# One residual sum moved from VectorE to TensorE and ScalarE in the last rows, and one bank read moved behind weight sums at the start

## The chip, the cores and the metric

The kernel runs on one core of one Trainium2 chip. The metric is device time in microseconds (us) of one execution; each kernel was run several times, and the profiles are of single executions on the same kind of chip. A profile's span is about 1.8 us shorter than the time that the same execution is given (2750.9 against 2752.65), so spans are compared with spans and times with times.

## The reference

128 graphs of 64 nodes with 768 features go through a layer norm and a ReLU, then two layers of attention over the graph, and the input is added at the end. Cut to what matters:

```python
h = jnp.maximum(_layernorm(x, axis=-1), 0.0)
for l in range(2):
    m_left  = jnp.einsum('bsh,oh->bso', h, W_left[l])
    m_right = jnp.einsum('bsh,oh->bso', h, W_right[l])
    u_left  = jnp.einsum('bih,bjh->bij', h, m_left) / temper
    u_right = jnp.einsum('bih,bjh->bij', h, m_right) / temper
    # ... choose left or right by the triangle, exp, mask, divide by the row sum -> attention
    h_lin = jnp.einsum('bsh,oh->bso', h, W_lin[l]) + b_lin[l]
    ctx   = jnp.matmul(attention, h_lin)
    h     = jax.nn.relu(_layer_norm(ctx, ln_a[l], ln_b[l]))   # (z - mu) / (sigma + eps) * a + b
return x + h                                                   # all float32
```

## The kernel before

Every big projection (768 x 768 weights) is done by fifteen block products in place of eighteen (3 x 3 weight blocks times 2 token halves): sums of weight blocks are multiplied with sums of token blocks, and each product is added with a sign into several blocks of the result. A bank (X, Y, Z, V or aux here) is a piece of PSUM, the memory that the products are written to. The graphs go through in blocks. At the very start the weight sums aren't ready, so block 0 makes them just in time on VectorE; the dictionary `just` says which sums are made after which product.

```python
def read(p, to, i, seen, copied=nc.scalar):        # PSUM bank -> result blocks of product i
    what = ORDER[i][3]
    for n in range(0, len(what), 2):
        sign, o = what[n], int(what[n + 1])
        if o not in seen:                            # first contribution: ScalarE copies
            seen.add(o)
            nc.scalar.activation(to(o), p, AF.Copy, scale=1.0 if sign == "+" else -1.0)   # [cut]
        else:                                        # later ones: VectorE adds
            added(nc.vector, to(o), sign, to(o), p)

# start of the program: GpSimd makes the first two weight sums, VectorE the others
for f in ws[:2]:
    f()
t, w = deque(sums_t((1, 0, 0), nc.vector)), deque(vs[2:])
needs = ("twtwt", "ttwww", "wwww", "w", "tw", "t", "ww", "ww", "tt", "", "tt")   # t: token sum, w: weight sum

def project(u, k, just):
    # [cut]
    for i, (at, t, _) in ...:                        # fifteen products
        # [cut: four matmuls, eight records in a trace, into bank `at`]
        read(p, lambda o: M[u][...], i, seen)
        for f in just.get(i, ()):
            f()
        run(30 * k + 2 * i + 1)
```

The second product (`i == 1`) goes to bank Z, and four sums ("wwww") follow its read in VectorE's queue.

The other place is the end. The last 256 rows are two tiles, k=1 and k=0, of 128 rows by 768 columns. For each, the context is normalised and clipped into `zs[k]`, added to the residual `xs[k]` (with the bias `b` already in it), and stored in two halves of 64 rows on two DMA queues.

```python
def finish_last(u, r):
    cx = context(u, r)                               # last products of the program, into PSUM
    # [cut]
    for k in (1, 0):
        nc.scalar.activation(squares[:, k]..., cx[k], AF.Square, accum_out=ss[k])
        nc.vector.tensor_tensor(zs[1 - k]..., cx[1 - k], rows["a"]..., op=ALU.mult)
        nc.scalar.activation(rs[k], ss[k], AF.Sqrt, bias=floor, scale=1.0 / (H - 1.0))
    for k in (1, 0):
        nc.vector.tensor_scalar_add(rs[k], rs[k], EPS_LN)
        nc.vector.reciprocal(rs[k], rs[k])
        nc.vector.scalar_tensor_tensor(zs[k], zs[k], rs[k], rows["-b"], op0=ALU.mult, op1=ALU.max)
        nc.vector.tensor_add(xs[k], xs[k], zs[k])
        for h, queue in enumerate((nc.sync, nc.scalar)):
            queue.dma_start(out[u * NBB + batch(r, k, h)], xs[k][h * S:(h + 1) * S])
```

Of the kernel before, what the change touches and what calls it, by code (L numbers as in the profile page):

```python
# [10 lines left out]
F32 = mybir.dt.float32  # L11
# [6 lines left out]
def kernel(  # L18
# [24 lines left out]
    nc = tc.nc  # L43
    B, S, H = x.shape
    L = w_lin.shape[0]
    P = 128
    C = H // P
    HH = H // 2
# [5 lines left out]
    TH = T // 2  # L54
# [10 lines left out]
    ps_st = ctx.enter_context(tc.tile_pool(name="ps_st", bufs=1, space=bass.MemoryType.PSUM))  # L65
# [11 lines left out]
    def put(slot, *fs):  # L77
        plan.setdefault(slot, []).extend(fs)
# [8 lines left out]
    def run(slot):  # L87
        if slot in plan:
            for f in plan.pop(slot):
                f()  # L90
        elif idle:
            f = idle.popleft()
            if f is not None:
                f()
# [59 lines left out]
    def added(eng, o, sign, a, b):  # L154
        (eng.tensor_add if sign == "+" else eng.tensor_sub)(o, a, b)  # L155
# [13 lines left out]
    def tokens_of(key):  # L169
        ht = HT[key]  # L170
        r = {f"B{2 * j + t}": ht[:, j * K2:(j + 1) * K2, t * TH:(t + 1) * TH] for j in range(3) for t in range(2)}
        r.update(TS.get(key, {}))
        return r
# [19 lines left out]
    def read(p, to, i, seen, copied=nc.scalar):  # L193
# [4 lines that stand above are left out]
            if o not in seen:  # L198
                seen.add(o)
                if copied is nc.vector:  # L200
                    nc.vector.tensor_scalar_mul(to(o), p, 1.0 if sign == "+" else -1.0)
                    continue
                nc.scalar.activation(to(o), p, AF.Copy, scale=1.0 if sign == "+" else -1.0)  # L203
            else:
                added(nc.vector, to(o), sign, to(o), p)
# [17 lines left out]
    KEEP = {}  # L223
# [168 lines left out]
    def pass_one(l, aside):  # L392
        with tc.tile_pool(name=f"one{l}", bufs=2, reuse_waits="tile") as sp:
# [26 lines left out]
            def project(u, k, just):  # L420


                b, w = lambda: tokens_of((1, l, u)), W[l, "lr"[k]]
                bank, seen = {}, set()


                ns = S - 1 if k and u < NB - 1 else S
                bs = "p (b s) -> p b s"
                for i, (at, t, _) in ((i, (o[1], o[2], o[3])) for i, o in enumerate(ORDER)):
                    new = i in FIRST  # L430
                    if new:
                        bank[at] = ps_st.tile([P, 2 * TH], F32, name=at)
                    p = bank[at][:, :NBB * ns].rearrange("p (g b s) -> p g b s", g=2, s=ns)
                    for g in range(2):
                        for c in range(K2):
                            nc.tensor.matmul(p[:, g], w[ORDER[i][0]][:, c, g * P:(g + 1) * P],  # L436
                                             b()[t][:, c, :].rearrange(bs, s=S)[:, :, :ns],
                                             start=(new and g == c == 0), stop=(c == K2 - 1), skip_group_check=True)
                        if g == 0:
                            run(30 * k + 2 * i)  # L440
                    if i == 0 and k == 0:
                        if u:
                            scores(u - 1)
                        M[u] = sp.tile([P, C, NBB, 2, S], F32, name="m", bufs=1)
                    read(p, lambda o: M[u][:, o // 2 * K2:(o // 2 + 1) * K2, o % 2 * 4:o % 2 * 4 + 4, k, :ns],
                         i, seen)
                    for f in just.get(i, ()):
                        f()
                    run(30 * k + 2 * i + 1)

# [53 lines left out]
            just = {}  # L504
# [130 lines left out]
    def pass_two(l, aside):  # L635
        last = l == L - 1
        with tc.tile_pool(name=f"two{l}", bufs=2, reuse_waits="tile") as sp:
# [12 lines left out]
            def context(u, r):  # L650


                hl, at = HL[u], AT[u]
                lo, hi = slice(0, S), slice(S, P)
                cx = [ps_aux.tile([P, 2, T], F32, name="aux") for _ in range(2)]
                for n in range(2):
                    for (j, k, i) in ((lo, 0, lo), (hi, 0, hi), (lo, 1, hi), (hi, 1, lo)):
                        q = r + 2 * k
                        m = n if j == lo else 1 - n
                        nc.tensor.matmul(cx[k][i, m, :HH], at[j, q, :], hl[j, q, m * HH:(m + 1) * HH],  # L660
                                         start=True, stop=True)
                return [c[:, :, :HH] for c in cx]
# [23 lines left out]
            def batch(r, k, h):  # L686
                return 4 * (h if k == 0 else 1 - h) + r + 2 * k
# [3 lines left out]
            def last_block(u):  # L691


                rest = big.tile([P, C, T], F32, name="ht").rearrange("p c t -> p (c t)")
                rows["-b"] = sp.tile([P, H], F32, name="nb", bufs=1)
                for r in range(2):
                    XS[u, r] = [rest[:, n * H:(n + 1) * H] for n in (2 * r, 2 * r + 1)]

                def load(r):
                    for k in range(2):  # L700
                        for h in range(PAIR):
                            nc.sync.dma_start(XS[u, r][k][h * S:(h + 1) * S], x[u * NBB + batch(r, k, h)])

                put(1, lambda: load(1))
                put(6, lambda: nc.gpsimd.tensor_scalar_mul(rows["-b"], rows["b"], -1.0))
                put(20, lambda: load(0))

                def offset():

                    t = stat.tile([P, 1], F32, name="hold", bufs=1)  # L710
                    nc.gpsimd.tensor_copy(t, XS[u - 1, 1][1][:, :1])
                    for xs in XS[u, 1]:
                        nc.gpsimd.tensor_add(xs, xs, rows["b"])

                put(42, offset)

            def finish_last(u, r):


                cx = context(u, r)  # L720
                zs = [sp.tile([P, H], F32, name="z", bufs=4) for _ in range(2)]
                squares = sp.tile([P, Q, H], F32, name="hl", bufs=2)
                two = "p (n d) -> p n d"
                xs = XS[u, r]
                of = stat.tile([P, 2, 2], F32, name="of", bufs=1)
                ss, rs = ([of[:, n, k:k + 1] for k in range(2)] for n in range(2))
                for k in (1, 0):
                    nc.scalar.activation(squares[:, k].rearrange(two, n=2), cx[k], AF.Square, accum_out=ss[k])
                    nc.vector.tensor_tensor(zs[1 - k].rearrange(two, n=2), cx[1 - k],
                                            rows["a"].rearrange(two, n=2), op=ALU.mult)  # L730
                    nc.scalar.activation(rs[k], ss[k], AF.Sqrt, bias=floor, scale=1.0 / (H - 1.0))
                for k in (1, 0):
                    nc.vector.tensor_scalar_add(rs[k], rs[k], EPS_LN)
                    nc.vector.reciprocal(rs[k], rs[k])
                    nc.vector.scalar_tensor_tensor(zs[k], zs[k], rs[k], rows["-b"], op0=ALU.mult, op1=ALU.max)
                    nc.vector.tensor_add(xs[k], xs[k], zs[k])
                    for h, queue in enumerate((nc.sync, nc.scalar)):
                        queue.dma_start(out[u * NBB + batch(r, k, h)], xs[k][h * S:(h + 1) * S])
                return []
# [134 lines left out]
            for u in range(NB):  # L874
# [21 lines left out]
                else:  # L896
                    if turn:
                        load_h(1, 1, 0)
                        put_all(28, affine(1, 1, 0), 3)
                        put_sums_t((1, 1, 0), 38, 2, 30)  # L900
                        ends = ({1: ((u - 1, 0), (13, 14, 16)), 11: ((u - 1, 1), (34, 35, 36))},
                                {4: ((u, 0), (50, 51, 52))})
                    else:
                        last_block(u)
                        put(8, lambda: residual(u - 1, 1))
                        ends = ({0: ((u - 1, 0), (12, 13, 15, 19, 31)), 9: ((u - 1, 1), (28, 29, 30, 39, 41))},
                                {2: ((u, 0), (44, 48, 51, 61, 62))})
# [54 lines left out]
```

## Time and profile before

| | before |
|---|---|
| time, median of 4 runs | 2751.59 us (2750.17 to 2751.72) |
| profiled span | 2750.9 us |
| TensorE idle before the fifth product of block 0 | 1.48 us |
| first product of block 0 to its fifth | 9.44 us |
| end of the last context product to end of the span (the tail) | 10.57 us |
| in the tail: tile 1's stores issued, VectorE done, last byte | 4.26, 6.54, 9.38 us from its start |

The profile is read as places. TensorE is busy in 99% of the span, so a change that doesn't touch TensorE's work can only win where TensorE is not busy. The busy time by stretches of the kernel before shows the two places of this change. The columns are the stretch in us from the span's start, its length, then the busy time (and the instructions) of TensorE, weight loads, VectorE, ScalarE and GpSimd, then the granted clock, the DMA share and GB/s:

```profile
12.80:72.00 59.20, 56.86 (x385) 49.39 (x386) 40.22 (x63) 19.21 (x37) 26.81 (x22) 1.00 0.70 187
...
2740.30:2750.90 10.60, 0.00 (x0) 0.00 (x0) 6.32 (x11) 2.28 (x6) 0.00 (x0) 0.68 0.56 148
```

The first row is the first block's projection: TensorE is idle for 2.3 of its 59.2 us. The second is the tail: TensorE does nothing, VectorE works for 6.3 of 10.6 us, the rest is waiting and transfers.

In a timeline line, the first two numbers are when a group of instructions starts and how long it lasts. Then come the engine (PE is TensorE, PEld its weight loads, DVE VectorE, ACT ScalarE, POOL GpSimd; SPq and ACTq are the stores and loads issued by SyncE and ScalarE), the source line, the operation, output and inputs, shapes and count; the bracket gives the idle time of that engine just before and what ended it. A line number such as L155 can be that of a helper that all sums share.

### The profile page before, as it was taken

To read this page: it belongs to the slowest core of one execution; us is meant where nothing else is said; L and a number is where in the kernel's file an instruction comes from. 1 tells how busy PE (TensorE), PEld (TensorE's weight loads), DVE (VectorE), ACT (ScalarE), POOL (GpSimd) and SP (SyncE) were. 2 spreads that over 40 slices of the span, in tenths; PEclk is the share of its full clock that TensorE was granted. 3 is DMA by queue.
4 is the path that set the end of the run, shared out by engine and by line. 5 is a ranking of instruction groups with operands and counts; after the bars stand their busy time and mean duration, and the time that the engine had idled before them with its cause. 6 is when DMAs were issued, how large, how long until landed. Compare 5 with 4: busy or idle time off the path is not lost.

```text
span 2750.9 us, 46440 instructions
## 1 busy us (share of the span) xinstructions
PE 2730.4 (99%) x18746; PEld 2343.1 (85%) x18746; DVE 1345.6 (49%) x2266; ACT 849.9 (31%) x1612; POOL 1194.4 (43%) x937
## 2 busy tenths in 40 slices
PE   9999999999999999999999999999999999999998
PEld 8888888888888888888788888888888888888886
DVE  6555445545454333333435444444444335666667
ACT  3222223222221154444621211121122214544443
POOL 3332452223223555555522444223222325887886
PEclk9999999999999999999999999999999999999999
DMA  7434433343332333343555433443344205555555
GB/s 206 118 75 98 123 80 81 91 120 89 76 79 74 102 106 119 119 146 127 150 128 148 100 76 76 109 118 79 76 97 120 61 26 146 161 169 167 169 165 150
DMA packets 234072, 310.82 MB, mean 113 GB/s; under 512 B 54146, under 2 KB 184450, under 8 KB 225666
## 3 DMA queue, kind: packets, MB, share of 16 engines
q1 hardware_dynamic: 233698, 307.45, 41.8%
q8 instruction: 149, 2.44, 0.4%
q14 instruction: 65, 0.53, 0.1%
q10 hardware_dynamic: 160, 0.39, 0.0%
HBM read 202.91 MB, written 104.86 MB: 112 GB/s over the span
## 4 chain that ended last, share of the span: by engine, by line
PE 97%; DVE 1%; ACT 1%; DMA 0%; issue 0%; SPq 0%; DVEq 0%; ACTq 0%
PE X L436 24%; PE V L436 16%; PE X L852 12%; PE Y L436 12%; PE Z L436 8%; PE V L852 8%; PE Y L852 6%; PE aux L463 5%; PE Z L852 4%; PE aux L660 2%; PE aux L683 1%; PE Y L683 0%; ACT xb L316 0%; DVE wm L477 0%; DMA w_l<-in_w_left_dram 0%
## 5 line engine op out<-in xcount | busy, mean ns | idle before, releaser
L155 POOL TENSOR_TENSOR ts<-ht 128x512 f32<-128x512 f32 x441 | 587.0, 1341 | 1223.6 <-DMA ht<-h 565.1
L203 ACT ACTIVATE m<-X 128x512 f32<-128x512 f32 (+1 forms) x256 | 151.6, 592 | 1087.6 <-PE X L436 569.7
L155 POOL TENSOR_TENSOR ts<-ht,ts 128x512 f32<-128x512 f32 x189 | 248.7, 1323 | 135.6 <-PE X L852 60.5
L155 DVE TENSOR_TENSOR m<-m,V 128x512 f32<-128x512 f32 (+1 forms) x256 | 173.3, 677 | 269.1 <-PE V L436 269.0
L155 DVE TENSOR_TENSOR m<-m,X 128x512 f32<-128x512 f32 (+1 forms) x256 | 162.9, 677 | 248.0 <-PE X L436 247.4
L852 PE MATMUL X<-w_n,ts 128*128 128x256 f32 x1024 | 244.3, 380 | 0.8 <-ACT hl L203 0.6
L436 PE MATMUL X<-ts,w_l 128*128 128x256 f32 x1024 | 242.7, 380 | 0.1
L436 PE MATMUL X<-ts,w_r 128*128 128x252 f32 (+1 forms) x1024 | 238.8, 376 | 0.0
L155 DVE TENSOR_TENSOR m<-m,Z 128x512 f32<-128x512 f32 (+1 forms) x128 | 87.5, 683 | 307.7 <-ACT m L203 248.9
L852 PEld LDWEIGHTS X<-w_n,ts 128*128 128x128 f32 x1024 | 191.5, 190 | 33.3 <-issue 3.6
L436 PEld LDWEIGHTS X<-ts,w_l 128*128 128x128 f32 x1024 | 192.0, 190 | 30.1 <-DVE m L155 2.7
L436 PEld LDWEIGHTS X<-ts,w_r 128*128 128x128 f32 x1024 | 192.0, 190 | 26.0
L275 ACT ACTIVATE ht<-ht,b_col,a_col 128x512 f32<-128x512 f32 x192 | 143.5, 804 | 148.8 <-DMA ht<-h 148.8
L852 PE MATMUL Y<-w_n,ts 128*128 128x256 f32 x768 | 182.5, 379 | 0.0
L436 PE MATMUL Y<-ts,w_l 128*128 128x256 f32 x768 | 181.5, 379 | 0.6 <-DVE w_l L155 0.6
L436 PE MATMUL Y<-ts,w_r 128*128 128x252 f32 (+1 forms) x768 | 179.1, 376 | 0.0
L436 PEld LDWEIGHTS Y<-ts,w_l 128*128 128x128 f32 x768 | 145.8, 190 | 20.8 <-DVE w_l L155 1.0
L852 PEld LDWEIGHTS Y<-w_n,ts 128*128 128x128 f32 x768 | 145.8, 190 | 20.4 <-issue 0.6
L436 PEld LDWEIGHTS Y<-ts,w_r 128*128 128x128 f32 x768 | 145.9, 190 | 17.4
L155 DVE TENSOR_TENSOR hl<-hl,V 128x512 f32<-128x512 f32 (+1 forms) x136 | 89.1, 655 | 129.6 <-PE V L852 112.0
L818 POOL TENSOR_TENSOR z<-z,b 128x768 f32<-128x768 f32 x62 | 112.6, 1828 | 76.2 <-DVE z L815 76.2
L203 ACT ACTIVATE hl<-X 128x512 f32<-128x512 f32 (+1 forms) x135 | 77.9, 577 | 219.4 <-PE X L852 216.5
(167 smaller groups left out, 4737.1 us busy)
## 6 DMA issues: line engine op xcount, KB each, us to landing
ht<-h SPq DMA_DIRECT2D x63, 1536.0 KB, 7.1
h<-xb SPq DMA_DIRECT2D x124, 384.0 KB, 6.0
z<-z SPq DMA_DIRECT2D x128, 192.0 KB, 3.1
x<-z SPq DMA_DIRECT2D x128, 192.0 KB, 8.4
x<-in_x_dram SPq DMA_DIRECT2D x120, 192.0 KB, 8.3
xr<-in_x_dram SPq DMA_DIRECT2D x120, 192.0 KB, 3.8
out_dram<-xr SPq DMA_DIRECT2D x120, 192.0 KB, 2.7
adj<-in_adj_dram SPq DMA_DIRECT2D x64, 128.0 KB, 2.7
```

Of the source, the lines that this page charges most:

```text
L155: (eng.tensor_add if sign == "+" else eng.tensor_sub)(o, a, b)
L203: nc.scalar.activation(to(o), p, AF.Copy, scale=1.0 if sign == "+" else -1.0)
L275: nc.scalar.activation(ht, ht, AF.Relu, bias=cols[1][:, c:c + 1], scale=cols[0][:, c:c + 1])
L436: nc.tensor.matmul(p[:, g], w[ORDER[i][0]][:, c, g * P:(g + 1) * P], b()[t][:, c, :].rearrange(bs, s=S)[:, :, :ns], start=(new and g == c ...
L463: nc.tensor.matmul(p[h * S + e:h * S + e + 32, q, e:e + 95], ht[:, c, b * S + e:b * S + e + 32], mb[:, e:e + 95], start=(c == 0), stop=(c ...
L660: nc.tensor.matmul(cx[k][i, m, :HH], at[j, q, :], hl[j, q, m * HH:(m + 1) * HH], start=True, stop=True)
L683: nc.tensor.matmul(parts[r, k][n][i], at[j, q, :], hl[j, q, cut], start=True, stop=True)
L818: nc.gpsimd.tensor_add(zs[k], zs[k], rows["b"])
L852: nc.tensor.matmul(p[:, n], b[t][:, c, r * P:(r + 1) * P], w[s][:, c, :], start=(i in FIRST and i not in PRELOAD and n == c == 0), stop=(c ...
```

## The change

Its intent: (1) at the start, let VectorE make the four sums for the fifth product before it reads bank Z, which nobody waits for; (2) in the tail, take tile 1's residual sum off VectorE, whose chain is the only one after the last product, and give it to TensorE (a product with the identity matrix, added to the residual that such a product has put into the bank earlier) and ScalarE (the copy out of the bank). GpSimd makes the identity again before the last block.

```diff
                         M[u] = sp.tile([P, C, NBB, 2, S], F32, name="m", bufs=1)
+                    sums = just.get(i, ())
+                    if i == 1:
+                        for f in sums:
+                            f()
+                        sums = ()
                     read(p, lambda o: M[u][:, o // 2 * K2:(o // 2 + 1) * K2, o % 2 * 4:o % 2 * 4 + 4, k, :ns],
                          i, seen)
-                    for f in just.get(i, ()):
+                    for f in sums:
                         f()
 # [cut]  last_block
                 rows["-b"] = sp.tile([P, H], F32, name="nb", bufs=1)
+                KEEP["ident"] = sp.tile([P, P], F32, name="ident", bufs=1)
+                make_identity(nc, KEEP["ident"])
 # [cut]  finish_last
+                total = [ps_st.tile([P, 2 * TH], F32, name=n) for n in "XY"]
+                half = [slice(n * HH, (n + 1) * HH) for n in range(2)]
+                for n in range(2):
+                    nc.tensor.matmul(total[n][:, :HH], KEEP["ident"], xs[1][:, half[n]], start=True, stop=False)
                 for k in (1, 0):
                     nc.vector.tensor_scalar_add(rs[k], rs[k], EPS_LN)
                     nc.vector.reciprocal(rs[k], rs[k])
                     nc.vector.scalar_tensor_tensor(zs[k], zs[k], rs[k], rows["-b"], op0=ALU.mult, op1=ALU.max)
-                    nc.vector.tensor_add(xs[k], xs[k], zs[k])
+                    if k:
+                        for n in range(2):
+                            nc.tensor.matmul(total[n][:, :HH], KEEP["ident"], zs[k][:, half[n]],
+                                             start=False, stop=True)
+                            nc.scalar.copy(xs[k][:, half[n]], total[n][:, :HH])
+                    else:
+                        nc.vector.tensor_add(xs[k], xs[k], zs[k])
                     for h, queue in enumerate((nc.sync, nc.scalar)):
                         queue.dma_start(out[u * NBB + batch(r, k, h)], xs[k][h * S:(h + 1) * S])
```

## The prediction

> **What bounds the kernel now.** I read the page first: the busy shares and the chain that ended last. They say that TensorE is the bound of nearly the whole run.
>
> ```profile
> PE 2730.4 (99%) x18746; PEld 2343.1 (85%) x18746; DVE 1345.6 (49%) x2266; ACT 849.9 (31%) x1612; POOL 1194.4 (43%) x937
> ...
> PE 97%; DVE 1%; ACT 1%; DMA 0%; issue 0%; SPq 0%; DVEq 0%; ACTq 0%
> ```
>
> So 2750.9 - 2730.4 = 20.5 us of the span is not TensorE. The busy time by stretches puts 3.1 us of that before 12.8 us, 2.3 us between 12.8 and 72 us, 4.5 us in all between 72 and 2740.3 us, and 10.6 us after the last product. The change touches two of these places and nothing else (the listed order of instructions on every engine differs only there). Even if both vanished, that is about half a per cent, so the question is one of tenths of a microsecond.
>
> The first place is read from the timeline of the first block, engine by engine.
>
> ```profile
> 18.73 0.68 DVE L155 TENSOR_TENSOR m<-m,Z 128x512 f32<-128x512 f32 x1
> 18.86 1.59 PEld L436 LDWEIGHTS Y<-ts,w_l 128*128 128x128 f32 x8 [0.98 <-DVE w_l L155]
> 18.86 1.99 PE L436 MATMUL Y<-ts,w_l 128*128 128x256 f32 x8 [0.58 <-DVE w_l L155]
> 19.32 3.47 DVE L155 TENSOR_TENSOR w_l<-w_l,w_l 128x512 f32<-128x512 f32 x5
> 22.30 1.59 PEld L436 LDWEIGHTS X<-ht,w_l 128*128 128x128 f32 x8 [1.85 <-issue]
> 22.34 1.97 PE L436 MATMUL X<-ht,w_l 128*128 128x256 f32 x8 [1.48 <-DVE w_l L155]
> ```
>
> The product at 22.34 is the fifth. TensorE sat idle 1.48 us for its weight sum. The first line, the read of the second product's bank Z, stands in VectorE's queue ahead of the four sums that the fifth product needs. The same stretch in the chain of waits shows that the fourth sum is what releases it, 0.14 us after its end:
>
> ```profile
> 21.50 0.70 DVE w_l L155
> 22.20 0.14 issue
> 22.34 1.97 PE X L436 x8
> ```
>
> The second place is the tail, from the timeline after the last product.
>
> ```profile
> 2739.81 0.48 PE L660 MATMUL aux<-hl,at 64*64 64x384 f32 x1
> ...
> 2742.51 1.02 DVE L735 SCALAR_TENSOR_TENSOR z<-z,of,nb 128x768 f32<-128x768 f32 x1
> 2743.57 0.96 DVE L736 TENSOR_TENSOR ht<-ht,z 128x768 f32<-128x768 f32 x1
> 2744.44 0.15 DVE L733 TENSOR_SCALAR of<-of 128x1 f32<-128x1 f32 x1
> 2744.55 2.78 SPq L738 DMA_DIRECT2D out_dram<-ht  x2
> 2744.55 2.81 ACTq L738 DMA_DIRECT2D out_dram<-ht  x2
> 2744.62 0.16 DVE L734 RECIPROCAL of<-of 128x1 f32<-128x1 f32 x1
> 2744.82 1.02 DVE L735 SCALAR_TENSOR_TENSOR z<-z,of,nb 128x768 f32<-128x768 f32 x1
> 2745.87 0.96 DVE L736 TENSOR_TENSOR ht<-ht,z 128x768 f32<-128x768 f32 x1
> ```
>
> VectorE finishes tile 1, then tile 0. Each tile leaves in two stores, one by SyncE's queue and one by ScalarE's. Tile 1's stores are issued at 2744.55, tile 0's after 2746.83. Busy time by stretches then shows when the bytes move:
>
> ```profile
> 2740.60:2744.00 3.40, 0.00 (x0) 0.00 (x0) 3.30 (x6) 2.01 (x6) 0.00 (x0) 1.00 0.85 231
> 2745.60:2747.40 1.80, 0.00 (x0) 0.00 (x0) 1.20 (x2) 0.00 (x0) 0.00 (x0) 0.50 0.83 219
> 2747.80:2749.70 1.90, 0.00 (x0) 0.00 (x0) 0.00 (x0) 0.00 (x0) 0.00 (x0) 0.50 0.79 207
> ```
>
> The last three numbers are the granted clock, the DMA share and GB/s. A pair (2 x 64x768 f32 = 0.393 MB) starts 1.05 us after its issue and takes some 1.7 us; the span ends 1.2 us after the last byte. The first row is the four stores of the rows before: 0.786 MB in 3.4 us.
>
> **What the Trainium skill says.** "FP8 and Floating Point Precision", TensorE Precision Notes: true FP32 takes 4 passes through the array. The trace agrees: each product of the program is two records, and eight 256-column records take 1.89 us with 0.38 us for one, so they start (1.89 - 0.38) / 7 = 0.215 us apart; that is 0.43 us, four times 256 columns at 2.4 GHz. "TensorE: Matmul & The Clock Gate", Part 1: after an idle window of some 3.4 us the array falls to half rate. The trace agrees: the clock falls from 1.00 to 0.50 at about 2744.1, 3.8 us after the last product. "DMA: Bandwidth & Descriptors", Issuing engines are not separate DMA queues: all issuers share the same 16 DMA engines. The trace agrees: a pair issued at once on two queues moves at 219 GB/s, no better than four stores of one queue at 231. "ScalarE: Activation LUTs", Table sets: the hidden batching unit: cheap functions, copy among them, are in every set. The trace agrees in that the table loads of the last pass stand at its first square root alone, though copies run throughout.
>
> **The change, part by part.** *Start.* The bank read moves behind four weight sums in VectorE's order. VectorE is busy without a break from 16.8 to 23.4 us, so nothing is saved there, but the sums start 19.32 - 18.73 = 0.59 us earlier, and so does the fifth product: idle 1.48 falls to about 0.89 us. Nothing else takes over that I can find: all nine weight loads had landed by 8.7 + 5.8 = 14.5 us (last issue and longest landing in the DMA issues), bank Z isn't written again until the fourteenth product, the sixth product's sum still ends at its old 22.8 us and is wanted at 23.5, the seventh's at 24.6 and wanted at 25.1. The rest of block 0 runs behind TensorE, so **0.59 us** should come through to the end.
>
> *Tail, taken off VectorE.* The 0.96 us addition of tile 1 goes. Tile 0's steps start at 2743.5 instead of 2744.44, and its addition ends at about 2745.88 instead of 2746.83: 0.95 us earlier.
>
> *Tail, added.* Two products of 384 columns add tile 1's rows to a bank early, right behind the last context products; nothing waits for them. Once z is there at 2743.53, two more must run. A 384-column record took 0.48 us; two records start 0.215 x 1.5 = 0.32 us apart. With 0.06 us for the first weight load, bank X is complete at 2743.53 + 0.05 + 0.06 + 0.32 + 0.48 = 2744.45 and bank Y 0.64 later, at 2745.1. A 128x384 copy by ScalarE took 0.46 to 0.49 us at the start of the run: the copies end at 2744.95 and 2745.6. So tile 1's stores leave at 2745.6, **1.05 us later** than now. Tile 0's are ready at 2745.88, but each queue is still issuing its first one (0.47 us on SyncE, some 0.53 on ScalarE, and issues follow each other at 0.57 to 0.6), so they leave at about 2746.15 to 2746.2, some 0.7 us earlier than now.
>
> *Tail, the sum.* The four stores now lie on each other. Data start at 2745.6 + 1.05 = 2746.65. Taken as two pairs of 1.7 us one behind the other they end at 2750.05; at the four-store rate of before (3.4 us) the same. Now the last byte moves at 2749.65. If the slow first half of a pair is paid once only, four stores could take some 2.7 us and end at 2749.35. So the tail gives between -0.4 and +0.3 us; I take **-0.1 us**, that is, the VectorE time saved is spent again on transfers that began later.
>
> The identity is built by GpSimd before the last block, about 0.5 us of it (0.20 and 0.29 at the start of the run). It stands beside sums that TensorE doesn't wait for there; the order has it behind the last of them. Sum: 0.59 - 0.1 = about 0.5 us.
>
> **Rivals.** (1) *The tail pays in full*: 0.95 us earlier, as VectorE's chain alone says, with 0.59 at the start: 2750.05. For it: VectorE is the only engine on the chain after 2740.5. Against it: tile 1's stores are pushed to the same moment, and 0.786 MB needs its 2.7 to 3.4 us from there. (2) *Half clock on the added products*: if the array is throttled when z comes at 2743.53, the records take twice as long, tile 1 leaves 0.6 to 1.3 us later still, and the tail loses about 1 us: 2752. Against it: the early products run until about 2741.7, so the idle stretch is 1.9 us and not 3.8. (3) *The start gains nothing*, because VectorE's later bank reads or ScalarE's work on block 1's rows hold TensorE at 40.1 us, where it waited 0.28 us already: 2751.7. Against it: that chain too begins behind TensorE's products.
>
> **Range and chances.** 2751.59 less 0.5 is 2751.1. The three runs before spread over 1.55 us with a mean of 2751.2, lower than their median, so I put the time at **2750.9**. The range takes in the rivals and that spread: 2749.5 to 2752.2. Two per cent are 55 us, more than all the time that isn't TensorE's: same 0.98, faster 0.01, slower 0.01.
>
> **What would show it.** The fifth product at about 21.75 us with an idle time near 0.9; the first product after it without a new wait; bank read of Z at about 21.5. In the tail: tile 0's addition ending about 0.95 us earlier measured from the last context product, ScalarE's copies ending 2 us after tile 1's z, four stores in one DMA stretch of 2.7 to 3.4 us, the granted clock 1.00 until the added products end. It is wrong if the tail from the last context product (now 10.6 us) shortens by more than 0.5 us or grows by more than 0.5, or if the time from the start to the second block doesn't shorten.

## The result, and the profile after

The changed kernel took 2751.14 us (median of 4 runs, 2750.94 to 2751.98) against 2751.59 (2750.17 to 2751.72). The ratio is 1.0 with a 95% interval of 0.9983 to 1.0017: the same. Here and below a ratio is the mean time of one kernel's fast runs over that of the other's of the same rounds, so it isn't quite the ratio of the medians quoted. The interval is some 4.7 us wide either way and the change is worth well under 1 us, so the times can't tell whether it helps. The traces have to.

| us | before | after |
|---|---|---|
| TensorE idle before the fifth product | 1.48 | 0.88 |
| first product of block 0 to its fifth | 9.44 | 8.85 |
| fifth product to the first score product after it (block 1) | 46.94 | 46.94 |
| tail | 10.57 | 10.72 |
| in the tail: tile 1's stores issued | 4.26 | 5.40 |
| VectorE done | 6.54 | 5.55 |
| tile 0's stores issued (SyncE, ScalarE) | 6.57, 6.57 | 5.99, 6.06 |
| first byte of the stores (before: tile 1's pair) | 5.39 | 6.55 |
| last byte | 9.38 | 9.33 |
| last byte to the end of the span | 1.19 | 1.40 |

(The rows from the tail on count from the end of the last context product.)

**The start.** The timeline of the first block of the kernel after:

```profile
16.67 4.79 DVE L155 TENSOR_TENSOR w_l<-w_l,w_l 128x512 f32<-128x512 f32 x7
...
21.38 0.68 DVE L155 TENSOR_TENSOR m<-m,Z 128x512 f32<-128x512 f32 x1
...
21.61 1.97 PE L436 MATMUL X<-ht,w_l 128*128 128x256 f32 x8 [0.88 <-DVE w_l L155]
23.41 1.89 PE L436 MATMUL V<-ht,w_l 128*128 128x256 f32 x8
```

VectorE now makes seven weight sums without a break, the read of Z stands behind them at 21.38, and the fifth product starts after 0.88 us of idle time in place of 1.48. The sixth follows at 23.41 with no bracket, so no wait took over there. The table's row from the fifth product to the scores, 46.94 us in both, says that nothing later in the block gave the gain back.

**The tail.** The timeline after the last context product (which ended at 2738.42) of the kernel after:

```profile
2738.35 0.91 PE L744 MATMUL X<-ht,ident 128*128 128x384 f32 x2
...
2740.64 1.02 DVE L748 SCALAR_TENSOR_TENSOR z<-z,of,nb 128x768 f32<-128x768 f32 x1
...
2741.72 0.91 PE L752 MATMUL X<-z,ident 128*128 128x384 f32 x2 [1.80 <-DVE of L746]
...
2742.71 0.48 ACT L754 COPY ht<-X 128x384 f32<-128x384 f32 x1 [1.91 <-PE X L752]
2743.01 0.96 DVE L756 TENSOR_TENSOR ht<-ht,z 128x768 f32<-128x768 f32 x1
2743.31 0.48 ACT L754 COPY ht<-Y 128x384 f32<-128x384 f32 x1
2743.82 1.43 ACTq L758 DMA_DIRECT2D out_dram<-ht  x2
2743.85 1.11 SPq L758 DMA_DIRECT2D out_dram<-ht  x2
```

Tile 1's z ends at 2741.66 and VectorE goes straight to tile 0. The two products and two copies of tile 1 end at 2743.79, that is 2.13 us later, so its stores are issued at 2743.82, only 0.15 us before VectorE ends tile 0 at 2743.97. The four stores now go out together: each queue issues its two within 1.1 and 1.4 us, where it took 2.8 before. Busy time by stretches, columns as in the same view of the kernel before:

```profile
2744.80:2746.20 1.40, 0.00 (x0) 0.00 (x0) 0.00 (x0) 0.00 (x0) 0.00 (x0) 0.95 0.86 193
2746.20:2747.80 1.60, 0.00 (x0) 0.00 (x0) 0.00 (x0) 0.00 (x0) 0.00 (x0) 0.50 0.85 323
2744.80:2747.70 2.90, 0.00 (x0) 0.00 (x0) 0.00 (x0) 0.00 (x0) 0.00 (x0) 0.72 0.88 271
2747.70:2749.10 1.40, 0.00 (x0) 0.00 (x0) 0.00 (x0) 0.00 (x0) 0.00 (x0) 0.50 0.00 0
```

One stretch (called the pile below) carries all four stores, slowly first (193 GB/s) and fast later (323). Its window is 2.9 us wide; from first to last byte 2.8 us pass, against 1.7 us for a pair of stores before. Then come 1.4 us without a byte until the end. Before, tile 1's pair went out during VectorE's work on tile 0, and only tile 0's pair lay at the end. VectorE is done 0.99 us earlier, and the last byte comes 0.05 us earlier.

**Why the times scatter more than the change is worth.** In block after block TensorE meets short waits before its small score products that the profile's list puts down to nothing it knows of ("issue"). The list of TensorE's waits (waiting line, releaser: us in total, times, longest us), of the kernel before and then of the kernel after:

```profile
PE aux L463 <- issue: 3.4, 7, 1.4
```

```profile
PE aux L470 <- issue: 1.9, 3, 1.4
```

They differ by 1.5 us in code that the change doesn't touch. Over eleven more runs (below) this entry had 4 to 9 times and 1.5 to 4.6 us. TensorE's whole idle time between the first projection product and the last context product was 6.80 us before, 5.08 after, and 4.6 to 8.6 in the runs below; that stretch less this idle time was 2720.5 to 2721.2 us in all thirteen. So these waits make a large part of the run-to-run spread, and the sizes of the change's parts are read from the places themselves. The DMA packets in the traces show what they follow. One line of the profile page's list of DMA queues (packets, MB, share of time), here of the kernel before, is:

```profile
q8 instruction: 149, 2.44, 0.4%
```

These are 149 packets of 16 KB of instructions. Each of the 86 waits of the thirteen runs ended 1.20 to 1.58 us after such a packet had ended, while only 3 to 4% of all TensorE records start 1.1 to 1.7 us after one. TensorE most likely waited for its own next instructions. No run moved these transfers to test it.

### The profile page after: what moved, and what is told of

Read it like the earlier page. It is cut to its first block, busy times and chain, and to the rows that moved or that the text cites. A ratio compares the mean times of both kernels' runs of the same rounds, so it can differ in the third digit from the quotient of the medians.

```text
span 2749.1 us, 46461 instructions
## 1 busy us (share of the span) xinstructions
PE 2732.7 (99%) x18754; PEld 2344.4 (85%) x18754; DVE 1344.6 (49%) x2265; ACT 850.8 (31%) x1614; POOL 1195.1 (43%) x939
## 4 chain that ended last, share of the span: by engine, by line
PE 97%; DVE 1%; ACT 1%; DMA 0%; issue 0%; SPq 0%; DVEq 0%; ACTq 0%
PE X L436 24%; PE V L436 16%; PE X L872 12%; PE Y L436 12%; PE Z L436 8%; PE V L872 8%; PE Y L872 6%; PE aux L470 5%; PE Z L872 4%; PE aux L667 2%; PE aux L690 1%; PE Y L690 0%; ACT xb L316 0%; DVE wm L484 0%; DMA w_l<-in_w_left_dram 0%
```

## The experiments

Two theories stood at first. Mine: the start gives 0.6 us; the tail gives nothing because the stores of tile 1, 1.1 us later than before, delay those of tile 0. The rivals: VectorE's chain sets the end of the tail, or the added wait for products and copies does, or the gain of the start is eaten later. Three sets of runs were made, each beside its own runs of the kernel before: median 2752.68 (9 runs, 2750.24 to 2753.61), 2751.76 (2751.17 to 2753.35) and 2752.18 (2751.72 to 2754.55).

### Each part alone

The start hunk of the diff alone, then the other hunks alone.

> The change at the start alone (bank read of Z behind the four weight sums; the tail as before). Theory: the start is worth 0.6 us and comes through whole: the fifth product idles 0.88 us instead of 1.48, the tail (from the last context product's end to the end of the span) stays at 10.6 us, the time is 0.6 us below before. Rival: a later wait of block 0 or 1 takes it back: idle before the fifth product 0.88 as well, but the first product of the second block starts no earlier relative to the first product of the first, and the time is that of before.

> The change at the tail alone. Theory: VectorE ends 0.99 us earlier, but tile 1's stores leave 1.1 us later and all four lie on each other, so the tail is 10.7 us against 10.57 of before and the time within 0.3 us of before. Rival: the tail's VectorE time pays and only the spread of the runs hid it: tail 9.6 us, time 1 us below before.

| | median us | ratio to before, 95% | idle before fifth | first to fifth | tail |
|---|---|---|---|---|---|
| start only | 2751.25 | 0.9997 (0.9985 to 1.001) | 0.88 | 8.86 | 10.56 |
| tail only | 2752.08 | 1.0 (0.9987 to 1.0014) | 1.48 | 9.45 | 10.56 |

The parts are independent: each shows its own landmark of the whole change and the other's of before. The start is worth 0.60 us. The tail part alone gives 10.56 against 10.57, and the whole change 10.72; its own second run (below) gave 10.64. So the tail is worth between +0.01 and -0.16, nothing to be told from its own spread of 0.16 us over these three runs.

### Without tile 1's stores

Is it tile 1's transfers that eat VectorE's 0.99 us? Here they are removed, in the kernel after and, as a control, in the kernel before. The result is wrong (rows of tile 1 aren't written).

```diff
+                        if k == 0:
                             queue.dma_start(out[u * NBB + batch(r, k, h)], xs[k][h * S:(h + 1) * S])
```

> The changed kernel with tile 1's two last stores left out (these rows of the output are wrong on purpose). Theory: the transfers of tile 1 are what tile 0's wait behind. Without them tile 0's stores leave 5.6 us after the last context product, their bytes move from 6.6 to 8.3, and the tail is 9.5 us instead of 10.7. Rival: the tail is set by something else at the end (landing and the closing barrier): it stays near 10.7, or falls only by the 0.45 us by which tile 0's stores are issued late.

> The kernel before with tile 1's two last stores left out (wrong on purpose), the control of the run above. Theory: in the kernel before tile 1's bytes have all moved before tile 0's begin (a gap of some 0.4 us between the two stretches), so leaving them out changes nothing: tail 10.57, time that of before. Rival: if any last store gains from a lone queue, the tail falls here too, by the same 1 us.

The times were 2751.72 (ratio 1.0, 0.9988 to 1.0013) and 2753.48 (1.0005, 0.9992 to 1.0018), of no use at this size. The tails were **9.71** us after (10.72 with the stores) and **10.70** before (10.57 with them). Timeline (one line) and stretches of the kernel after without these stores:

```profile
2745.45 0.47 SPq L759 DMA_DIRECT2D out_dram<-ht  x1
```

```profile
2746.60:2748.40 1.80, 0.00 (x0) 0.00 (x0) 0.00 (x0) 0.00 (x0) 0.00 (x0) 0.60 0.80 212
2748.40:2749.60 1.20, 0.00 (x0) 0.00 (x0) 0.00 (x0) 0.00 (x0) 0.00 (x0) 0.50 0.00 0
```

Tile 0's store goes out at 2745.45, right at VectorE's end; its pair alone takes 1.7 us from first to last byte where the pile took 2.8. So the 0.99 us is really there in VectorE's chain and comes through to the end in full (10.70 - 9.71) if nothing of tile 1 stands in the way. In the kernel before, tile 1's stores cost nothing. This excludes the rival that the products and copies themselves delay tile 0, and leaves tile 1's stores. They hold tile 0 in two ways that this run removes together: their issues (tile 0's stores leave at 5.58 without them, at 5.99 and 6.06 with them) and their bytes. The tail fell by 1.0 us, more than the 0.45 us of the issues.

### Tile 1 earlier by splitting its scaling; tile 1 first; both

If the start of the pile sets the end, tile 1's stores must leave earlier, even at VectorE's expense. Splitting z of tile 1 into column halves lets the first product start half a z earlier:

```diff
-                    nc.vector.scalar_tensor_tensor(zs[k], zs[k], rs[k], rows["-b"], op0=ALU.mult, op1=ALU.max)
+                    if not k:
+                        nc.vector.scalar_tensor_tensor(zs[k], zs[k], rs[k], rows["-b"], op0=ALU.mult, op1=ALU.max)
                     if k:
                         for n in range(2):
+                            nc.vector.scalar_tensor_tensor(zs[k][:, half[n]], zs[k][:, half[n]], rs[k],
+                                                           rows["-b"][:, half[n]], op0=ALU.mult, op1=ALU.max)
```

> The changed kernel with tile 1's scaling and maximum cut into two halves of 384 columns, each product going out behind its half: tile 1's stores leave earlier (4.75 us after the last context product instead of 5.40), VectorE's chain to tile 0 is some 0.1 us longer. Theory (the end is set by when the pile of four stores starts: first issue plus 5.28 us in the changed kernel): tail 10.05 us against 10.68, although VectorE ends later. Rival (tile 0's own stores set the end): tail 10.7 to 10.8.

Measured: 2750.91 us, ratio 0.9996 (0.9983 to 1.001), tail **10.32**. From its timeline:

```profile
2741.02 1.15 DVE L753 SCALAR_TENSOR_TENSOR z<-z,of,nb 128x384 f32<-128x384 f32 x2
...
2743.52 0.96 DVE L759 TENSOR_TENSOR ht<-ht,z 128x768 f32<-128x768 f32 x1
2743.80 1.43 ACTq L761 DMA_DIRECT2D out_dram<-ht  x2
```

The two halves take 1.15 us where the whole took 1.02, so VectorE ends 0.13 us later (at 5.68 us from the tail's start); the stores are issued at 5.00 us and not 5.40 (4.75 was put), and the tail shortens by 0.40. The tail follows the stores, not VectorE's end. This run alone doesn't say which stores, since tile 0's left earlier too (both at 5.71, after 5.99 and 6.06). The next one does.

The counter-test delays VectorE's end and leaves tile 1's stores: tile 0's multiplication by `a` is moved out of the square loop to stand behind tile 1's scaling.

```diff
                 for k in (1, 0):   # squares
-                    nc.vector.tensor_tensor(zs[1 - k].rearrange(two, n=2), cx[1 - k],
-                                            rows["a"].rearrange(two, n=2), op=ALU.mult)
 # [cut]
                 for k in (1, 0):   # scaling
+                    nc.vector.tensor_tensor(zs[k].rearrange(two, n=2), cx[k],
+                                            rows["a"].rearrange(two, n=2), op=ALU.mult)
                     nc.vector.tensor_scalar_add(rs[k], rs[k], EPS_LN)
```

> The changed kernel with VectorE's multiplication by the row a of tile 0 moved behind tile 1's scaling, so that tile 1 is ready as soon as its deviation is: tile 1's stores leave at 4.8 us after the last context product, tile 0's at 6.0 instead of 5.6. Theory: the end is the later of first issue plus 5.28 and tile 0's issue plus 4.15 (the tail without tile 1's stores less its issue), both 10.1: tail 10.1 us. Rival (the chain of VectorE sets the end): tail 11.1 us.

Measured: 2751.27 us, ratio 0.9999, tail **10.61**. From its timeline:

```profile
2741.12 0.96 DVE L744 TENSOR_TENSOR z<-aux,a 128x768 f32<-128x768 f32 x1 [0.79 <-ACT hl L737]
...
2745.61 0.96 DVE L756 TENSOR_TENSOR ht<-ht,z 128x768 f32<-128x768 f32 x1
```

I had meant tile 1's z to come earlier too; that missed. The first line's bracket says that VectorE waited 0.79 us for ScalarE's square of the same bank, as the Trainium skill, "PSUM — Partial Sum Buffer", section "PSUM bank collisions raise a hardware error", has it: the compiler's scheduler makes two engines that touch one bank and one quarter of the partitions wait for each other, two reads too. So tile 1's stores leave at 5.40 us as in the kernel after, VectorE ends 0.87 us later, at 6.42, and the tail is as long as ever (10.64 and 10.72). This excludes the rivals that in the changed kernel VectorE's chain, or the issue of tile 0's stores (now 6.44), sets the end: both came later and the tail didn't. The delay used up all the slack, for by the two bounds below this run's end is reached by either (5.40 + 5.2, 6.44 + 4.2).

Both edits together:

> Both of the edits above: tile 1's stores leave at about 4.3 us, tile 0's at 6.1. Theory: now tile 0's stores are the later bound, 6.1 plus 4.15: tail 10.2 us, no better than either alone. Rival (the first issue alone sets the end): tail 9.6 us.

Measured: 2751.42 us, ratio 0.9998, tail **10.76**, with the first issue at 5.00 us, VectorE done at 6.54 and tile 0's stores issued at 6.57. The tail that was put, 10.2, missed because both issue times did (4.3 and 6.1 were put); the rule itself, tile 0's issue plus 4.15, gives 10.72. Now the earlier start of the pile no longer helps, because tile 0's own stores leave as late as in the kernel before.

The runs agree on two bounds, and the tail is the later of the two: the first store's issue plus 5.2 to 5.3 us when the four stores pile up (after: 10.72 - 5.40, second run 10.64 - 5.40; split: 10.32 - 5.00), or tile 0's issue plus 4.0 to 4.2 us (before: 10.57 - 6.57; without tile 1's stores 9.71 - 5.58 and 10.70 - 6.57). Both sizes are fitted to these runs. The kernel before lay on the second; the change moved it to the first, at the same length.

### Tile 1 stored in halves of columns

If the pile must start earlier still, tile 1's first half can leave after the first copy. SyncE's queue takes the first half, ScalarE's the second:

```diff
                             nc.scalar.copy(xs[k][:, half[n]], total[n][:, :HH])
+                            for h in range(PAIR):
+                                (nc.sync, nc.scalar)[n].dma_start(out[u * NBB + batch(r, k, h)][:, half[n]],
+                                                                  xs[k][h * S:(h + 1) * S, half[n]])
```

(on top of the split scaling; tile 0 as before).

> The split scaling, and tile 1 stored in column halves, the first half on SyncE's queue right behind its copy. The pile of stores starts at about 4.4 us after the last context product instead of 5.0, tile 0's at 5.7 (SyncE) and 6.1 (ScalarE, behind its two issues). Theory: now tile 0's stores set the end: tail about 9.9 us against 10.3. Rival: rows of 1536 bytes instead of 3072 and six issues instead of four cost what the earlier start gives: tail 10.3 us or more.

Measured: 2751.95 us, ratio 0.9997, tail **10.44**, against 10.32 without it: a miss. From its timeline, the stores on each queue:

```profile
2744.11 1.11 SPq L759 DMA_DIRECT2D out_dram<-ht  x2
...
2745.42 0.47 SPq L764 DMA_DIRECT2D out_dram<-ht  x1
...
2746.25 0.59 ACTq L764 DMA_DIRECT2D out_dram<-ht  x1
```

The pile starts at 4.39 us from the tail's start, but ScalarE's queue must issue two halves of tile 1 first, and tile 0's second store leaves at 6.53, 0.83 us after its twin on SyncE. That store is most likely the bound: 6.53 + 3.9 = 10.44. So three stores issued one behind the other on ScalarE would have cost what the earlier start gave; the shorter rows of the rival weren't tested apart from it.

### GpSimd makes one more sum at the start

On top of the split scaling, GpSimd takes the sum of weights 6 and 10 from VectorE, so that the fifth product should hardly wait at all:

```diff
-                for f in ws[:2]:
+                for f in ws[:2] + ws[7:8]:
-                t, w = deque(sums_t((1, 0, 0), nc.vector)), deque(vs[2:])
+                t, w = deque(sums_t((1, 0, 0), nc.vector)), deque(vs[2:7] + vs[8:])
-                needs = ("twtwt", "ttwww", "wwww", ...)
+                needs = ("twtwt", "ttwww", "www", ...)
```

> The kernel of the split scaling with, at the start, one of the four sums ahead of the fifth product given to GpSimd, which is idle there from 11.9 us. Theory (the fifth product waits for VectorE's queue alone, so one sum less is worth its 0.72 us): idle before the fifth product 0.16 to 0.2 us instead of 0.88. Rival (GpSimd's sum slows VectorE's operations beside it, as VectorE's sums took 1.16 and 1.37 us instead of 0.68 beside GpSimd's at 38 to 41 us): the fourth product comes some 0.6 us later and the gain is gone.

Measured: 2751.01 us, ratio 0.9996 (0.9983 to 1.0008), tail 10.32. From its timeline:

```profile
13.97 1.27 POOL L155 TENSOR_TENSOR w_l<-w_l,w_l 128x512 f32<-128x512 f32 x1 [1.62 <-DMA w_l<-in_w_left_dram]
...
14.33 1.46 DVE L155 TENSOR_TENSOR ts<-ht 128x512 f32<-128x512 f32 x1 [0.35 <-ACT ht L362]
...
20.30 1.99 PE L436 MATMUL Y<-ts,w_l 128*128 128x256 f32 x8 [0.74 <-DVE w_l L155]
...
22.45 1.97 PE L436 MATMUL X<-ht,w_l 128*128 128x256 f32 x8 [0.15 <-DVE w_l L155]
```

The fifth product waits 0.15 us in place of 0.88, as hoped, yet the first product to the fifth takes 8.90 us against 8.85: no gain. A token sum of VectorE beside GpSimd's sum took 1.46 us where one alone takes 0.68, and ended 0.55 us after GpSimd's. The second product now waits 0.35 us where it had not waited, and the fourth longer (0.74 against 0.59 in the split version). GpSimd's sum stood just there because it had itself waited 1.62 us for its weights (first line). That VectorE was held is what the Trainium skill says in "SBUF — State Buffer", section "Who interferes with whom": a VectorE instruction with two inputs in SBUF and a GpSimd instruction that reads SBUF exclude each other. The run agrees with it; a second sum of 1.48 us beside a GpSimd sum stands in the run with half stores.

### The best version and the change, once more

> The split scaling again, for the time on one chip with the changed kernel and with before: tail 10.30 us as in its first run, TensorE idle before the fifth product 0.88 us; time 0.9 us below before by the sum of both places (0.6 and 0.3), and 0.35 below the changed kernel. The spread of single runs is 1.5 to 3 us, so the times may not tell them apart; the two landmarks will.

> The changed kernel again, unaltered, on the same chip: tail 10.68 us within 0.1, idle before the fifth product 0.88 us, time 0.5 us below before. If the tail differs by more than 0.15 us between two runs of one kernel, the landmarks are not as firm as the readings take them.

| | median us | ratio to before, 95% | tail |
|---|---|---|---|
| start and split scaling, again | 2751.17 | 0.9996 (0.9983 to 1.0008) | 10.25 |
| the change, again | 2751.29 | 0.9996 (0.9983 to 1.0008) | 10.64 |

The tails repeat within 0.1 us. By the landmarks the version with split scaling is 0.2 to 0.5 us better than the change and some 0.9 better than before (0.60 at the start and 0.25 to 0.32 in the tail). The times don't show it, since every interval holds 1. And a place can be disturbed: in this second run of the split version the idle time before the fifth product was 0.88 again, but from the first product to it 9.68 us passed, as a weight load landed late and the second and fourth products waited 0.40 and 0.74 us. Over the three sets, the kernels with the start hunk had means 0.1 to 1.2 us below that of the kernel before in the same set, and the two without it means 0.3 and 1.2 us above. That fits a gain of 0.6, but is too coarse to prove it; in the runs of the result itself the two means were equal (2751.30 with the change, 2751.27 without).

## Why the prediction was right

The time came out at 2751.14 us where 2750.9 was put, in its range, and the same within 2%. But a range 2.7 us wide on a kernel that scatters by 1.5 is no test of its steps, and that the median fell by 0.45 us where 0.5 was put is luck: the means of the same runs differ by 0.03 us, the other way. The traces test the steps.

- **TensorE bounds the run, and only two places matter.** Held: both parts left the rest of the run alone, and the time between the first projection product and the last context product, once idle time is taken off, was 2720.6 us before and after (2720.5 to 2721.2 in all runs). GpSimd's identity (0.20 and 0.29 us, at 2711.4 us) held nothing up.
- **The start, 0.59 us from the length of the bank read.** Measured 0.60 (idle 0.88 where 0.89 was put). The fifth product stood at 21.61 and the read of Z at 21.38, where 21.75 and 21.5 were put. No new wait followed, and the old one of 0.28 us that the third rival names stayed at 0.28, so the rival that the start gains nothing is excluded.
- **VectorE's end, 0.95 us earlier.** Measured 0.99.
- **Tile 1's stores, 1.05 us later.** Measured 1.14: the copies end 2.13 us after z, where 2 was put. Tile 0's left 0.5 to 0.6 us earlier, where 0.7 was put.
- **No half clock for the added products.** Held: the granted clock stayed at 1.00 until they ended and fell at about 2746.0. They came 1.80 us after the early ones; the rival of 2752 us is excluded. The argument against it was less safe than it looked: the 3.8 us that the prediction read was one draw. Over the thirteen profiled runs the clock fell 2.25 to 5.07 us after TensorE's last product.
- **The tail, -0.1 us, because the time saved on VectorE is spent on transfers that start later.** Measured between -0.01 and +0.16. That tile 1's stores are the reason is shown by taking them out (10.72 to 9.71 after, no gain before), and by moving the two ends in the split and tile-1-first runs. The rival in which the tail pays in full would be right for a kernel without those stores.
- **Mis-sized inside that sum.** The -0.1 was taken from the middle of two cases, and it came near because errors cancelled.
  - A pair's first byte comes 1.13 us after SyncE's issue, not 1.05 as read from the edge of a window.
  - As the main case I let the four stores run for 3.4 us, two pairs one behind the other, and named 2.7 as the other way; they took 2.8. The 219 to 231 GB/s that I took for their rate was no ceiling: the later part of the pile moved at 323.
  - The slow beginning is SyncE's queue moving alone. ScalarE's first byte came 1.02 to 1.03 us after SyncE's in twelve runs (1.00 in the half stores), in a pair and in the pile alike. Why it starts late is open.
  - I hadn't put down the time from the last byte to the end at all: it was 1.40 and 1.35 us and not 1.19, which gave 0.2 back. The difference lies before the last store is signalled as landed (0.35 us after its last byte before, 0.55 and 0.51 after); from there to the end it was 0.84 us in both.

What remains open is why a few of the 149 instruction transfers are followed by a wait and most aren't; these waits scatter more from run to run than the whole change is worth.

## What to carry to other kernels

Where the end of a kernel is a compute chain followed by stores, ask when the first byte can go, not only when the last engine is done: freeing an engine by a detour that makes the earlier tile late piles its transfer onto the last one, and the gain is gone. In a just-in-time start, put what the next product waits for ahead of the reads that nobody waits for; here that gave 0.60 us and no new wait. And where a change is smaller than the run-to-run spread, judge it by the same landmark in each trace, a control and a counter-test, since the times won't tell.

## What the Trainium skill lacked or had wrong

- "DMA: Bandwidth & Descriptors": it has rates by size for loads on GpSimd's queue, but no word on how a short burst of stores from the queues of SyncE and ScalarE builds up. Here a lone pair of 192 KB stores took 1.7 us and four piled up took 2.8; in the first 1.02 us of either only SyncE's bytes moved, though both queues were issued to at once.
- The same page, in the table at its head, has some 0.6 us to the first byte for these queues, without saying from when. For SyncE's store these runs show 1.13 us from the start of the issue and 0.66 from its end; for ScalarE's, issued at the same moment, 2.15 to 2.19 from the start.
- "SBUF — State Buffer", section "Who interferes with whom", gives the rule of exclusion that the runs agree with, but no size for this pair: a 128x512 sum on VectorE grew from 0.68 to 1.46 us beside one of GpSimd, and ended 0.55 us after it.
- "TensorE: Matmul & The Clock Gate", Part 1, has the clock fall after an idle window of some 3.4 us. Here it fell 2.25 to 5.07 us after the last product in thirteen runs.
- "Runtime: NRT & Kernel Launch", section "Instruction fetch mechanics", has the cost of crossing a 16 KiB block of instructions as mostly hidden. The waits of TensorE that follow such transfers came 3 to 9 times in a run, up to 1.5 us each, 1.5 to 4.6 us in sum, all ahead of runs of small products (here 128x95).
